# A convolution network on one core: the order of the shifted copies, and when their split is issued

## The chip, the cores and the metric

The kernel runs on one core of a Trainium2 chip. The metric is the device time of one execution in microseconds (us). Five engines matter here: TensorE (PE; its weight loads are shown as PEld), VectorE (DVE), ScalarE (ACT), GpSimd (POOL) and SyncE (SP), which issues most of the transfers. Each engine works through its own queue in order.

## The reference

Four layers, each `x = x + layer(group_norm(x))` on an image batch of 4 x 32 x 32 x 16. Layers 0, 1 and 3 are the same construction with other weights: every output position has a 3x3 convolution kernel of its own, whose result over the whole image is compared with the input and summed with weights.

```python
first = einsum('ijyx,byxc->bijc', M, inputs)
kern = transpose(G, (0, 1, 5, 4, 2, 3)).reshape(h * w * f, c, 3, 3)
shifted = conv(x_nchw, kern, 'SAME')            # 1024 positions x 16 channels, each a 32 x 32 image
diff = relu(inputs[:, None, None] - shifted)
second = einsum('ijyx,bijyxc->bijc', W, diff)
return first - second
```

Layer 2 pools intervals of the image and runs two small steps of a dynamic programme with sigmoids. It is cheap beside the others.

## The kernel before

**Phases and steps.** The batch is taken in two groups `g` of two images (`GB = 2`). The three convolution layers and two groups make six phases; layer 3 of the reference is layer index 2 of the kernel, and layer 2 of the reference is worked (`interval_layer`) inside the preparation of that one. A phase has 8 chunks of 128 output positions, and a chunk 32 steps, one for each of 16 filters and 2 images: 256 steps a phase, 1536 in all. In a step, `first_part` runs 8 matmuls into a PSUM pair (four such pairs rotate), ScalarE scales it (L614), `second_part` of the step before runs 6 more matmuls, and VectorE takes the minimum with 0, multiplies by the weights W and sums (L630).

**Precision in parts.** Weights and inputs are split into a high part and a rest, so that products keep more digits: `iy`, `iz` and `iyz` are the parts of the input for taps 0 to 7, `im9` (im in the profile) is the input for tap 8. `split` makes them: VectorE cuts the high part of both slots (`upper`, L191, upper_x in the profile), GpSimd subtracts it (L259), ScalarE scales it (L263); then `halve` (L167, ScalarE), two `difference` (L266, GpSimd) and `halve_rest` (L170, VectorE) follow.

**Weights.** `prep_parts` prepares one unit (4 filters of a chunk) in every 8 steps, spread over places 0 to 7: at place 0 the high part (VectorE L191), at 1 the ninth tap's half (ScalarE L167), at 2 L224 on ScalarE with L225 and L226 on GpSimd, at 3 L228 and L229, at 4 the next unit's subtraction (GpSimd L202), at 6 the two transfers L235, which copy the parts turned to the other half of the partitions, and the load of another unit (L107). L235 and L107 are on SyncE's queue.

**What runs behind.** The generator `behind(phase)` prepares the next phase while the current one runs: the group norm, the write of the normalised image into a padded buffer `xs` in DRAM (L346, four transfers), the shifted copies `raw` out of it (L356: 12 taps or rows, two transfers each), a wait, then the split. Slots 0 and 1 of `raw` hold taps 0 to 7, 16 partitions each for either half of the image; slot 2 holds tap 8 four times over. A positive number that the generator yields is a number of steps to wait. `IDLE` (0) waits for a step whose place in the unit allows it (0, 4, 5, 6, 7), `CALM` for place 5, 6 or 7. The order of all instructions is written out in this way; the scheduler doesn't change it. In phases 0 and 2 the split is followed by `first_terms`, 128 matmuls for the first sum of a layer (L386) and their addition. Whatever is left of `behind` at the end of a phase is issued at once.

The places where this preparation runs are reached at step 102 of phase 0 (first shifted copy), at step 38 of phases 1 and 2, and at step 210 of phases 3 and 4, where the interval layer comes first. The wait ahead of the split is 12 steps in phases 0 to 2 and 7 in phases 3 and 4.

Of the kernel before, what the change touches and what calls it, by code (L numbers as in the profile page):

```python
# [41 lines left out]
def net_kernel(ctx: ExitStack, tc: tile.TileContext, x, xq, xi, convs, iv_w, iv_b, out):  # L42
# [123 lines left out]
    def halve(dst, src, mask):  # L166
        nc.scalar.activation(dst, src, AF.Copy, scale=mask[:, 1:2])  # L167

    def halve_rest(dst, src, mask):
        nc.vector.scalar_tensor_tensor(  # L170
            dst, src, mask[:, 0:1], dst.bitcast(F32), op0=ALU.mult, op1=ALU.add
        )
# [11 lines left out]
    def image(v, x):  # L184
        return v.rearrange("... (y x) -> ... y x", x=x)[..., :H]
# [68 lines left out]
    def split(eng, g, b, name, pause=IDLE):  # L254

        high = upper(image(raw[:, :2, b], HP), 2, f"x{name}{b}")
        yield 1
        for s in range(2):
            eng.tensor_tensor(  # L259
                image(iz[g][:, s, b], H), image(raw[:, s, b], HP), image(high[:, s], H), ALU.subtract  # L260
            )
            yield pause
            nc.scalar.activation(iy[g][:, s, b], high[:, s], AF.Copy, scale=EPS)  # L263

    def difference(eng, g, b, s):
        eng.tensor_tensor(  # L266
            iyz[g][:, s, b], iy[g].bitcast(F32)[:, s, b], iz[g].bitcast(F32)[:, s, b],
            ALU.subtract,
        )
# [64 lines left out]
    def before_conv(g, layer):  # L334
        xn = work.tile([P, NT, GC], F32, tag="xn", bufs=2, name=f"xn_{g}_{layer}")
        xns[g] = xn
        yield from group_norm(g, f"c{g}{layer}", xn, 1 if layer == 2 else 4)

        nc.vector.transpose(
            xt[g][:, :, 1 : 1 + H], xn
        )
        inner = xs[g][:, HP : HP + H * HP].rearrange("p (t r n) -> p r t n", r=ROWS, n=HP)
        for r in range(ROWS):
            nc.sync.dma_start(inner[:, r], xt[g][GC * r : GC * (r + 1)])  # L346
        yield 2
        xsv = xs[g].rearrange("(b c) n -> c b n", b=GB)
        at = 0
        for slot, row, tap in [(2, row, 8) for row in range(4)] + [  # L350
            (tap // 4, tap % 4, tap) for tap in range(8)
        ]:
            for h in range(2):
                off = (HI * h + tap // 3) * HP + tap % 3
                r0 = 64 * h + C * row
                nc.sync.dma_start(  # L356
                    raw[r0 : r0 + C, slot ^ h if slot < 2 else 2, :, :RUN], xsv[:, :, off : off + RUN]
                )
            at += 1
            if at % 3 == 0:  # L360
                yield 1
        yield 7 if layer == 2 else 12
        for b in range(GB):
            yield from split(nc.gpsimd, g, b, f"{g}{layer}")
            yield IDLE
            halve(image(im9[g][:, b], H), image(raw[:, 2, b], HP), low_x)
            for s in range(2):
                difference(nc.gpsimd, g, b, s)
            yield 3
            halve_rest(image(im9[g][:, b], H), image(raw[:, 2, b], HP), low_x)  # L370
            yield 1
# [309 lines left out]
    def behind(phase):  # L681
        g, layer = phases[phase]
        if phase == 0:
            yield from rest_of_start()
            nc.scalar.dma_start(X[1], x[1])
            zeros(1)
            yield 1
            yield from constants()
        if phase + 1 < len(phases):
            g1, layer1 = phases[phase + 1]  # L690
            if layer1 == 2:
                yield from interval_layer(g1)
            terms = g1 == NG - 1 and layer1 < NL - 1
            if terms:
                mt = load_first_terms(layer1)
            yield from before_conv(g1, layer1)
            if terms:
                yield from first_terms(layer1, mt)
        if phase == len(phases) - 1:
            mt = load_first_terms(layer)  # L700
            yield 24
            yield from first_terms(layer, mt)
            yield 4
            nc.sync.dma_start(out[1 - g], X[1 - g])
# [228 lines left out]
```

## Time and profile before

| | |
|---|---|
| median of three runs | 2592.98 us (2589.51 to 2595.02) |
| the profiled execution | 2596.07 us, of it the span of the profile 2594.3 us |
| mean granted TensorE clock | 0.996 |
| matmuls of the convolutions, L584 | 394 ns each as shown, overlapping in the array |
| L630 on VectorE | 1536 x 1224 ns |
| L614 on ScalarE | 1520 x 1008 ns |
| L225, L229, L226, L202 on GpSimd, each x190 | 1293, 1302, 1292, 1051 ns |
| L259, L266 on GpSimd (split), each x20 | 1206, 1301 ns (medians) |
| L235 transfers, x380 | 384 KB, 5.0 us from issue to landing (median) |
| L356 transfers, x120 | 67.8 KB, 2.4 us from issue to landing (median) |
| first L356 of each preparation | at 187.67, 514.47, 936.55, 1654.22 and 2086.48 us |

The span is what the profiler sees, from the first instruction to the last; the execution's own time is 1.8 us longer. A busy TensorE is not TensorE at its peak, since matmuls overlap: what counts is how many of them fall into a stretch. Where the profile says that an engine waited for another, the wait stands in brackets behind the instruction, with the idle time before it. SPq is SyncE's queue issuing a transfer; the number beside it is how long the issue held the queue. The profile strips numbers from names, so raw stands for the weight loads `raw_<n>` and for the shifted copies; the line tells them apart.

### The profile page before, as it was taken

To read this page: it belongs to the slowest core of one execution; us is meant where nothing else is said; L and a number is where in the kernel's file an instruction comes from. 1 tells how busy PE (TensorE), PEld (TensorE's weight loads), DVE (VectorE), ACT (ScalarE), POOL (GpSimd) and SP (SyncE) were. 2 spreads that over 40 slices of the span, in tenths; PEclk is the share of its full clock that TensorE was granted. 3 is DMA by queue.
4 is the path that set the end of the run, shared out by engine and by line. 5 is a ranking of instruction groups with operands and counts; after the bars stand their busy time and mean duration, and the time that the engine had idled before them with its cause. 6 is when DMAs were issued, how large, how long until landed. Compare 5 with 4: busy or idle time off the path is not lost.

```text
span 2594.3 us, 56641 instructions
## 1 busy us (share of the span) xinstructions
PE 2564.1 (99%) x21906; PEld 2117.6 (82%) x21906; DVE 2080.3 (80%) x3620; ACT 1894.2 (73%) x2169; POOL 1102.6 (43%) x990
## 2 busy tenths in 40 slices
PE   8999999999999999999999999999999999999999
PEld 5997888888888887888888877798888789788887
DVE  8886777877777877777788878788888877777777
ACT  4776777777777776777777777777777777677776
POOL 3444333453333344333345554454646353333332
PEclk9999999999999999999999999999999999999999
DMA  5655444454444654444444444544444466444442
GB/s 168 185 145 143 131 131 134 121 154 130 129 137 129 195 158 111 137 129 129 131 139 131 131 124 133 151 131 124 125 132 134 127 148 195 119 139 131 131 131 52
DMA packets 81182, 353.80 MB, mean 136 GB/s; under 512 B 18448, under 2 KB 20368, under 8 KB 80144
## 3 DMA queue, kind: packets, MB, share of 16 engines
q1 hardware_dynamic: 79920, 349.57, 48.2%
q8 instruction: 172, 2.82, 0.4%
q14 instruction: 98, 0.80, 0.1%
q10 hardware_dynamic: 864, 0.58, 0.1%
q0 software_dynamic: 128, 0.02, 0.0%
HBM read 199.19 MB, written 0.98 MB: 77 GB/s over the span
## 4 chain that ended last, share of the span: by engine, by line
PE 95%; DMA 2%; issue 1%; SPq 1%; ACT 0%; POOL 0%; DVE 0%; POOLq 0%; DVEq 0%; ACTq 0%
PE pc L584 93%; DMA parts<-parts 1%; PE pf L386 1%; DMA raw<-in_g 1%; SPq L356 1%; ACT pc L614 0%; POOL parts L225 0%; POOL W L226 0%; PE ps_l L509 0%; SPq L235 0%; DVE junk L630 0%; PE ps_r L522 0%; SPq L346 0%; DMA raw<-xs 0%; POOL parts L229 0%
## 5 line engine op out<-in xcount | busy, mean ns | idle before, releaser
L630 DVE SCALAR_TENSOR_TENSOR junk<-pc,WT 128x1024 f32<-128x1024 f32 x1536 | 1879.9, 1224 | 485.0 <-PE pc L584 437.6
L614 ACT ACTIVATE pc<-pc 128x1024 f32<-128x1024 f32 x1520 | 1531.8, 1008 | 664.1 <-PE pc L584 631.0
L584 PE MATMUL pc<-iy,parts 64*128 64x512 f32 x6080 | 1063.4, 394 | 13.7 <-DMA parts<-parts 13.6
L584 PE MATMUL pc<-iyz,parts 64*128 64x512 f32 x6080 | 1059.8, 394 | 4.0 <-ACT pc L614 4.0
L584 PE MATMUL pc<-iz,parts 64*128 64x512 f32 x6080 | 1059.8, 393 | 0.0
L584 PEld LDWEIGHTS pc<-iy,parts 64*128 64x128 f32 x6080 | 664.5, 185 | 140.8 <-DMA parts<-parts 17.2
L584 PEld LDWEIGHTS pc<-iz,parts 64*128 64x128 f32 x6080 | 665.2, 185 | 121.2
L584 PEld LDWEIGHTS pc<-iyz,parts 64*128 64x128 f32 x6080 | 645.7, 185 | 111.7 <-ACT pc L614 3.7
L584 PE MATMUL pc<-im,W 64*128 64x512 f32 x3072 | 714.8, 397 | 0.0
L225 POOL TENSOR_TENSOR parts<-raw,upper_w 128x512 fp32r<-128x512 f32 x190 | 245.7, 1293 | 1091.2 <-PE pc L584 955.3
L584 PEld LDWEIGHTS pc<-im,W 64*128 64x128 f32 x3072 | 372.4, 185 | 64.0 <-issue 3.6
L229 POOL TENSOR_TENSOR parts<-parts 128x512 fp32r<-128x512 f32 x190 | 247.3, 1302 | 2.2 <-ACT parts L224 1.6
L226 POOL TENSOR_TENSOR W<-W,raw 128x512 fp32r<-128x512 f32 x190 | 245.5, 1292 | 4.6 <-ACT W L167 4.6
L202 POOL TENSOR_TENSOR raw<-raw,ident 128x512 f32<-128x512 f32 x190 | 199.6, 1051 | 60.9 <-DMA raw<-in_g 39.5
L167 ACT ACTIVATE W<-raw,low_w 128x512 fp32r<-128x512 f32 x190 | 136.1, 716 | 0.1
L630 DVE DVE_READ_ACCUMULATOR junk<-pc,WT 128x1 f32 x1536 | 127.5, 83 | 0.0
L224 ACT ACTIVATE parts<-upper_w 128x512 fp32r<-128x512 f32 x190 | 118.6, 624 | 4.2 <-DVE upper_w L191 4.2
L228 ACT CAST parts<-upper_w 128x512 fp32r<-128x512 f32 x190 | 116.7, 614 | 0.0
L191 DVE TENSOR_SCALAR upper_w<-raw 128x512 int32<-128x512 int32 x190 | 82.0, 432 | 0.0
L645 POOL TENSOR_SCALAR acc<-acc 128x32 f32<-128x32 f32 x40 | 11.5, 288 | 160.4 <-DVE junk L630 155.8
L541 POOL TENSOR_TENSOR tables<-ft_b,rt 128x1089 f32<-128x1089 f32 x16 | 37.7, 2354 | 0.4 <-DVE s_b L548 0.4
L541 POOL TENSOR_TENSOR tables<-ft_a,rt 128x1089 f32<-128x1089 f32 x16 | 37.6, 2351 | 0.0
(137 smaller groups left out, 393.0 us busy)
## 6 DMA issues: line engine op xcount, KB each, us to landing
raw<-in_g SPq DMA_DIRECT2D x190, 768.0 KB, 7.2
parts<-parts SPq DMA_DIRECT2D x380, 384.0 KB, 5.0
WT<-in_w SPq DMA_DIRECT2D x48, 512.0 KB, 4.4
MT<-in_mt SPq DMA_DIRECT2D x6, 2048.0 KB, 14.0
raw<-xs SPq DMA_DIRECT2D x120, 67.8 KB, 2.4
raw<-in_xi SPq DMA_DIRECT2D x3, 271.0 KB, 4.6
raw<-in_xi SPq DMA_DIRECT2D x1, 813.0 KB, 7.2
xs<-xt SPq DMA_DIRECT2D x20, 34.0 KB, 2.0
```

What stands on the lines that cost most here:

```text
L167: nc.scalar.activation(dst, src, AF.Copy, scale=mask[:, 1:2])
L191: nc.vector.tensor_scalar(t.bitcast(I32), src.bitcast(I32), HIGH, None, op0=ALU.bitwise_and)
L202: eng.tensor_tensor(raws[u][:, s, at:to], raws[u][:, s, at:to], pick[s][:, f0 + at : f0 + to].unsqueeze(2).to_broadcast([P, to - at, P]), ...
L224: nc.scalar.activation(WD, high, AF.Copy, scale=-EPS)
L225: nc.gpsimd.tensor_tensor(WL, w8, high, ALU.subtract)
L226: nc.gpsimd.tensor_tensor(W9, W9.bitcast(F32), src[:, 2], ALU.add)
L228: nc.scalar.copy(WU, high)
L229: nc.gpsimd.tensor_tensor(WD, WD.bitcast(F32), WL.bitcast(F32), ALU.add)
L541: nc.gpsimd.tensor_tensor(t, ft[:, i, :].unsqueeze(1).to_broadcast([P, T1, T1]), rt, ALU.add,)
L584: nc.tensor.matmul(ps[:, h, :], lhsT=w[r], rhs=v[r], start=first and k == 0, stop=k == len(pairs) - 1, skip_group_check=not first,)
L614: nc.scalar.activation(ps, ps, AF.Copy, scale=1.0 + EPS)
L630: nc.vector.scalar_tensor_tensor(junk, ps.rearrange("p h n -> p (h n)"), 0.0, chunks[n], op0=ALU.min, op1=ALU.mult, accum_out=accs[phase][ ...
```

## The change

The list of shifted copies is put in another order: taps 0 to 7 come first, and the four rows of tap 8 last. The number of transfers and the yields between them stay. The wait between the last of them and the first split becomes 12 steps instead of 7 in layer index 2, and 24 instead of 12 in the others. Nothing else is touched.

```diff
         xsv = xs[g].rearrange("(b c) n -> c b n", b=GB)
         at = 0
-        for slot, row, tap in [(2, row, 8) for row in range(4)] + [
-            (tap // 4, tap % 4, tap) for tap in range(8)
+        for slot, row, tap in [(tap // 4, tap % 4, tap) for tap in range(8)] + [
+            (2, row, 8) for row in range(4)
         ]:
             for h in range(2):
                 off = (HI * h + tap // 3) * HP + tap % 3
...
             at += 1
             if at % 3 == 0:
                 yield 1
-        yield 7 if layer == 2 else 12
+        yield 12 if layer == 2 else 24
         for b in range(GB):
             yield from split(nc.gpsimd, g, b, f"{g}{layer}")
             yield IDLE
```

## The prediction

> **What bounds the kernel now.** I read the page's busy times first, then the chain that ended last, then the busy times in 20 us windows, and then each engine's timeline around the five places where a phase's input is prepared (I call them turns: phase 1's input is prepared in phase 0, and so on up to phase 5's).
>
> From the page: TensorE is busy for all but 30 us, and the chain is its work.
>
> ```profile
> PE 2564.1 (99%) x21906; PEld 2117.6 (82%) x21906; DVE 2080.3 (80%) x3620; ACT 1894.2 (73%) x2169; POOL 1102.6 (43%) x990
> PE 95%; DMA 2%; issue 1%; SPq 1%; ACT 0%; POOL 0%; DVE 0%; POOLq 0%; DVEq 0%; ACTq 0%
> ```
>
> The windows (start:end, length, then PE busy and its matmuls, PEld, DVE, ACT, POOL, PE clock, DMA share, GB/s) show where it loses time: a full window holds 174 to 176 matmuls, the ones at the turns fewer, and the window after turn 1's stall is full.
>
> ```profile
> 180.00:200.00 20.00, 20.00 (x174) 18.38 (x172) 16.26 (x29) 15.86 (x19) 8.62 (x8) 1.00 0.45 105
> 200.00:220.00 20.00, 17.23 (x125) 13.93 (x123) 11.26 (x19) 10.37 (x12) 6.22 (x6) 0.83 0.62 167
> 220.00:240.00 20.00, 20.00 (x174) 17.51 (x172) 17.39 (x29) 17.98 (x23) 14.82 (x14) 1.00 0.55 166
> ...
> 1660.00:1680.00 20.00, 16.35 (x127) 12.58 (x125) 11.87 (x21) 11.83 (x14) 6.30 (x6) 0.93 0.74 186
> 1680.00:1700.00 20.00, 20.00 (x171) 17.93 (x171) 16.94 (x29) 16.75 (x21) 16.95 (x16) 0.99 0.50 146
> ```
>
> TensorE's timeline, from one group of products to the same of the next step, has a regular step of 1.63 us. Above it I find, in order of the turns: 5.15, 2.99 and 2.47; 3.72, 2.70 and 2.10; 4.63; 6.06 and 2.93; 6.10, 2.98 and 2.37. The excess over 1.63 is 5.7, 3.6, 3.0, 5.7 and 6.6 us: 24.6 us, nearly all that could be won outside the start and the end.
>
> What stalls it there is SyncE's queue. Its timeline in turn 1:
>
> ```profile
> 184.02 1.81 SPq L346 DMA_DIRECT2D xs<-xt  x4
> 187.67 8.23 SPq L356 DMA_DIRECT2D raw<-xs  x18
> 196.06 1.10 SPq L235 DMA_DIRECT2D parts<-parts  x2
> 197.21 1.25 SPq L107 DMA_DIRECT2D raw<-in_g  x1
> 198.51 5.33 SPq L356 DMA_DIRECT2D raw<-xs  x6
> ```
>
> The two L235 transfers turn a unit's weight parts over to the other half of the partitions. POOL had finished their source at 184.74 (L229 began at 183.44, 1.30 long), but they stand behind eighteen of the shifted copies and start at 196.06. They land at 203.51, and TensorE waits:
>
> ```profile
> 203.51 0.79 PE L584 MATMUL pc<-iy,parts 64*128 64x512 f32 x1 [2.77 <-DMA parts<-parts]
> ```
>
> In turn 4 the order is the same: all 24 copies (15.07 us of queue), then L235.
>
> **What the Trainium skill says.** "DMA: Bandwidth & Descriptors", section "Anatomy of one DMA", says that the transfer engines don't wait on semaphores: a wait is made by the issuing sequencer, before dispatch. So what stands behind a copy in SyncE's queue waits with it, as the 11.3 us of L235 here show. "TensorE: Matmul & The Clock Gate", Part 1, says that the array's clock is halved after idleness and comes back after about 3.4 us of work, in a window that runs freely. The trace agrees with the halving: steps of 2.70 to 2.99 us follow four of the stalls, and turn 3's 3.0 us stall is followed by none. "SBUF — State Buffer", "Who interferes with whom", makes VectorE and GpSimd exclude each other on a shared port; the im correction L170 (748 ns at best, 1815 ns at most) is the operation that shows it.
>
> **Part 1: the order of the taps.** Twelve taps with two transfers each are issued before and after, with a yield after every third. Each transfer writes 16 partitions (67.8 KB). Whatever its tap, a group of four goes through the rows 0, 1, 2, 3 (tap 8's four copies, taps 0 to 3, taps 4 to 7), so with tap 8 moved from first to last the sequence of partition blocks and sizes stays the same; only the slot and the source offset differ. All of them wait for the same thing (the four xs writes; 5.3 us in 3 turns). So SyncE's queue up to and with L235 is unchanged, at 0.42 us a copy plus its gap, and so are the five stalls. Cost 0. What does change is which consumer's data lands first: the split (slots 0 and 1) can start eight copies earlier, 8 x 0.466 = 3.7 us (the chain has one copy every 0.466 us), and the im copies read data that land last. In VectorE's queue the im correction now has waits of its own for tap 8, which the split's wait covered before: up to 8 semaphore instructions of about 28 ns (the median of such an instruction on L356), 0.2 us once a turn. VectorE has 1.63 - 1.31 = 0.32 us free in each step, and TensorE's four PSUM pairs let it be a step late: hidden.
>
> **Part 2: the longer wait.** I count the steps from the yields. A unit's weights take eight steps (places 0 to 7); an IDLE yield waits for places 0, 4, 5, 6 or 7. In turn 1 the first split moves from step 118 to 130 of its phase, in turns 2 and 3 from 54 to 66, in turns 4 and 5 from 221 to 226. The whole preparation ends at steps 148, 84 and 244 instead of 133, 69 and 236. All are below 256, so nothing is left over to be issued at once at the end of a phase; turns 4 and 5 keep 12 steps, 20 us, before the next phase reads their result.
>
> What the wait removes: in turns 4 and 5 the split is issued before its data are there, and VectorE, queued in order, stands still:
>
> ```profile
> 1671.39 0.69 DVE L191 TENSOR_SCALAR upper_x<-raw 128x1024 int32<-128x1024 int32 x1 [0.88 <-DMA raw<-xs]
> 2104.46 0.69 DVE L191 TENSOR_SCALAR upper_x<-raw 128x1024 int32<-128x1024 int32 x1 [2.27 <-DMA raw<-xs]
> ```
>
> Both go, 3.15 us of VectorE. But TensorE has stalled on L235 at 1672.7 and 2104.4 in any case, until 1676.82 and 2108.34, with VectorE's next products late behind it. Value 0. At most, if these holds do lengthen the last two stalls, they come down to the mean of the first three (4.1 us): 1.6 + 2.5 = 4.1 us gained. Not below that, for turns 1 to 3 have such stalls without any split near them.
>
> What it adds is another position. Before, turns 1 to 3 run a split at places 3 to 7, turns 4 and 5 at 2 to 6. After, the second image runs at 2 to 6 in all five. The first image takes its high part at place 7, its first subtraction (POOL, 1.20 us) at place 0 ahead of the next unit's L225, and then waits for place 4: iy at 4 and 5, im at 6. POOL has 4.9 us of weights and 2 x 1.2 + 2 x 1.3 = 5.0 us of split in 13.1 us, and the weights have 10 us to spare before TensorE needs them (184.74 to 200.24, less 5.0 us for the median landing): hidden. ScalarE is tighter. Its eviction (1.01 us, one each 0.92 us when back to back, with 0.62 us idle) leaves room for one 0.62 us operation per step. The weights fill places 1 to 3, the split now fills 4 to 6: six steps in a row, two of them 0.72 us. Turn 4's second image in the trace has just that pattern; the worst step of TensorE beside it is 1.71 us instead of 1.63, and turn 5's is 1.70. I take 0.07 us for each of ten images, 0.7 us, against 0.3 us of such slips now: +0.4 us.
>
> **Part 3: what follows the split.** In phases 0 and 2 the first terms (128 matmuls, 7.04 us) come 15 steps later. They are TensorE's own work in a queue with work before and behind; their weights were loaded long before. They end well ahead of the next phase's norm. Cost 0.
>
> Sum on the profiled execution: 2594.3 + 0.4 = 2594.7 us of span (2596.5 with the 1.8 us around it). The runs' median stands 3.1 us lower at 2592.98, so **2593.4 us**.
>
> **Rivals.**
> - *The holds matter* (8%): turns 4 and 5 lose their extra, 2593.0 - 4.1 = 2588.9 us. For it: they are longer stalls and hold the waits. Against it: turn 1's is as long as turn 4's, without a split near.
> - *The queue comes free* (6%): the new order lets L235 start in time, all five stalls go: 2593.0 - 24.6 = 2568.4 us. Against it: the number of copies ahead of L235 is the same.
> - *ScalarE falls behind* (12%), the slower one: six filled steps in a row leave ScalarE more than its 0.62 us late, TensorE waits for the eviction, and the clock drops for a step. One such step costs 2.99 - 1.63 = 1.36 us; with ten images 13.6 us: 2606.6 us. It decides from half a microsecond an image. For it: TensorE already waits for ScalarE six times (4.0 us). Against it: the same pattern cost 0.08 us in turn 4.
> - *Nothing that counts* (74%): 2593.4 us.
>
> **Numbers.** The before runs spread over 5.5 us, so less than about 0.2% (5.2 us) can't be told from no change. The second rival counts as faster; of the first, 3 in 100 fall beyond 0.2% and 5 within. Faster 0.09, same 0.79, slower 0.12. The range, 2588 to 2599, takes in the gain of the holds nearly whole, the run spread, and the beginning of ScalarE's case.
>
> **What would show it.** L356 is still 18 plus 6 (or 24) ahead of L235, with steps of 3.7 to 6.1 us on TensorE at the same five places; upper_x no longer waits for raw<-xs; L202 in turns 4 and 5 is no longer behind a subtraction; steps beside the splits stay below 1.75 us. I'm wrong if TensorE has new steps over 2 us some 20 us after a stall (ScalarE's or POOL's case), or if L235 starts earlier than 11 us after its source in turn 1.

## The result and the profile after

The changed kernel takes 2593.72 us (median of 12 runs, 2589.41 to 2597.91) beside 2591.49 us for the kernel before on the same chips (12 runs, 2588.86 to 2595.02). The ratio is 1.0007 with a 95% interval of 0.9998 to 1.0016: no change that can be told from none. The forecast was 2593.4 us; that it lies 0.3 us from the median is luck, since runs of one kernel lie up to 8.5 us apart.

The page and the 20 us windows of the changed kernel (start:end, length, then PE busy and its matmuls, PEld, DVE, ACT, POOL, PE clock, DMA share, GB/s):

```profile
PE 2564.2 (99%) x21906; PEld 2158.5 (83%) x21906; DVE 2084.0 (80%) x3620; ACT 1893.7 (73%) x2169; POOL 1101.9 (42%) x990
...
180.00:200.00 20.00, 20.00 (x174) 18.39 (x172) 16.29 (x28) 15.70 (x19) 8.78 (x8) 1.00 0.45 108
200.00:220.00 20.00, 17.03 (x131) 13.76 (x129) 11.56 (x21) 10.93 (x13) 5.84 (x5) 0.91 0.70 182
220.00:240.00 20.00, 20.00 (x176) 17.31 (x174) 15.98 (x27) 14.81 (x17) 6.74 (x8) 1.00 0.52 155
1660.00:1680.00 20.00, 16.83 (x129) 12.99 (x127) 11.46 (x20) 10.80 (x13) 5.31 (x5) 0.90 0.71 178
```

The hole at 200 to 220 us is there as before, 131 matmuls (125 before) where a full window has 174 to 176, and so is the one of turn 4. The window after it, 220 to 240, has lost the split: GpSimd's busy time there fell from 14.82 to 6.74 us. TensorE had no use for that. SyncE's timeline of turn 1 says why the hole stays:

```profile
184.18 1.81 SPq L346 DMA_DIRECT2D xs<-xt  x4
187.95 8.23 SPq L356 DMA_DIRECT2D raw<-xs  x18
196.34 1.11 SPq L235 DMA_DIRECT2D parts<-parts  x2
197.49 1.32 SPq L107 DMA_DIRECT2D raw<-in_g  x1
```

Eighteen copies in 8.23 us, to the hundredth what it was, then L235. Its source was finished at 184.90 (L229, 183.60 plus 1.30), so the parts start 11.4 us late, and TensorE waits:

```profile
204.00 0.49 PE L584 MATMUL pc<-iy,parts 64*128 64x512 f32 x1 [2.97 <-DMA parts<-parts]
```

In the same reading of TensorE's steps as in the prediction, the excess over 1.63 us at the five turns is 5.0, 1.5, 6.1, 6.4 and 5.7 us, 24.6 us in all before rounding. That this is the sum of before to the tenth is a coincidence: each turn's own share is another, and the sum varies by several us between executions. What did change is VectorE. The high part no longer waits; its two instructions of turns 4 and 5 stand without a bracket, behind the stall:

```profile
1685.52 0.69 DVE L191 TENSOR_SCALAR upper_x<-raw 128x1024 int32<-128x1024 int32 x1
...
2117.20 0.69 DVE L191 TENSOR_SCALAR upper_x<-raw 128x1024 int32<-128x1024 int32 x1
```

### The profile page after: what moved, and what is told of

Read it like the earlier page. It is cut to its first block, busy times and chain, and to the rows that moved or that the text cites. A ratio compares the mean times of both kernels' runs of the same rounds, so it can differ in the third digit from the quotient of the medians.

```text
span 2594.4 us, 56655 instructions
## 1 busy us (share of the span) xinstructions
PE 2564.2 (99%) x21906; PEld 2158.5 (83%) x21906; DVE 2084.0 (80%) x3620; ACT 1893.7 (73%) x2169; POOL 1101.9 (42%) x990
## 4 chain that ended last, share of the span: by engine, by line
PE 94%; DMA 2%; issue 1%; SPq 1%; DVE 0%; ACT 0%; POOL 0%; ACTq 0%; DVEq 0%; POOLq 0%
PE pc L584 93%; DMA parts<-parts 1%; PE pf L386 1%; SPq L356 1%; DMA raw<-in_g 0%; DMA raw<-in_xi 0%; ACT pc L614 0%; DVE junk L630 0%; DMA first<-in_g 0%; POOL parts L225 0%; PE ps_l L509 0%; SPq L346 0%; POOL W L226 0%; SPq L235 0%; PE ps_r L522 0%
## 5 line engine op out<-in xcount | busy, mean ns | idle before, releaser
L614 ACT ACTIVATE pc<-pc 128x1024 f32<-128x1024 f32 x1520 | 1531.8, 1008 | 665.1 <-PE pc L584 640.1
L584 PE MATMUL pc<-iy,parts 64*128 64x512 f32 x6080 | 1074.4, 394 | 13.5 <-DMA parts<-parts 13.5
L584 PE MATMUL pc<-iyz,parts 64*128 64x512 f32 x6080 | 1070.8, 394 | 4.0 <-ACT pc L614 4.0
L584 PE MATMUL pc<-iz,parts 64*128 64x512 f32 x6080 | 1070.6, 393 | 0.0
L584 PEld LDWEIGHTS pc<-iy,parts 64*128 64x128 f32 x6080 | 681.0, 185 | 129.0 <-DMA parts<-parts 17.0
L584 PEld LDWEIGHTS pc<-iz,parts 64*128 64x128 f32 x6080 | 681.5, 185 | 109.3
L584 PEld LDWEIGHTS pc<-iyz,parts 64*128 64x128 f32 x6080 | 660.3, 185 | 100.1 <-ACT pc L614 3.9
L584 PE MATMUL pc<-im,W 64*128 64x512 f32 x3072 | 725.4, 397 | 0.0
L584 PEld LDWEIGHTS pc<-im,W 64*128 64x128 f32 x3072 | 382.7, 185 | 57.9 <-issue 3.4
L229 POOL TENSOR_TENSOR parts<-parts 128x512 fp32r<-128x512 f32 x190 | 246.7, 1298 | 2.0 <-ACT parts L224 1.6
## 6 DMA issues: line engine op xcount, KB each, us to landing
MT<-in_mt SPq DMA_DIRECT2D x6, 2048.0 KB, 13.4
```

The lines of the kernel that those rows point to most:

```text
L229: nc.gpsimd.tensor_tensor(WD, WD.bitcast(F32), WL.bitcast(F32), ALU.add)
L584: nc.tensor.matmul(ps[:, h, :], lhsT=w[r], rhs=v[r], start=first and k == 0, stop=k == len(pairs) - 1, skip_group_check=not first,)
L614: nc.scalar.activation(ps, ps, AF.Copy, scale=1.0 + EPS)
```

## The experiments

The theory was that the shifted copies in SyncE's queue, ahead of the weight parts, set the stalls, and that neither the order nor the longer wait touches that queue. The rivals: two effects that cancel; VectorE's holds; the load on the transfer rings rather than the queue. The kernel before ran again beside each group of experiments: its median was 2590.38 us beside the first four (25 runs), 2590.49 us beside the lumped copies and the two short waits (9 runs), and 2591.65 us beside the last pair (23 runs). Ratios are against these.

**Each part alone.** `e1_order` is the changed list with the old waits, `e2_wait` the old list with the new waits.

```diff
# e1_order, against the changed kernel
-        yield 12 if layer == 2 else 24
+        yield 7 if layer == 2 else 12
# e2_wait, against the kernel before
-        yield 7 if layer == 2 else 12
+        yield 12 if layer == 2 else 24
```

> The new order of the taps with the waits of before (12 and 7 steps). Theory A (the issue of the copies on SyncE's queue ahead of the weight parts sets the stalls, and neither part of the change touches it): same as before, ratio 1.000 within 0.001, about 2591.5 us; five stalls at the turns of some 25 us in all; the two holds of VectorE on the high part in turns 4 and 5 (0.88 and 2.27 us before) shrink to nothing, since slots 0 and 1 land eight copies earlier. Rival B (the two parts of the change have effects of a few us that cancel): 1 to 4 us faster or slower than before, and the wait alone the other way.

> The old order of the taps with the longer waits (24 and 12 steps). Theory A: same as before, ratio 1.000 within 0.001, five stalls of some 25 us in all, no hold of VectorE on the shifted copies, TensorE's steps beside the splits at most 1.71 us. Rival B: off by 1 to 4 us, the other way than the order alone.

Measured: 2592.26 us, ratio 1.0006 (0.9997 to 1.0014), and 2593.68 us, ratio 1.0007 (0.9999 to 1.0015). Each is within what can be told from nothing, and neither goes the other way: nothing cancels. All three medians (both parts, order, wait) do lie above their own before, by 2.2, 1.9 and 3.3 us, so a cost of some 2 us isn't excluded; the three traces don't show where it would lie, for none has more stall than the profile of before. Either part alone takes away the holds on the high part in turns 4 and 5. With the order alone the instruction of turn 4 starts 16.21 us after the first copy of its turn (1652.26 to 1668.47) instead of 17.17 us (1654.22 to 1671.39): earlier by about the 0.88 us of the hold, since its eight taps are no longer the last to land. The steps beside the splits with the wait alone were 1.71 us at most, as expected. The stalls were 21.8 and 20.6 us, somewhat smaller in these two executions.

**The queue, spread.** The one edit is a yield after every tap.

```diff
             at += 1
-            if at % 3 == 0:
-                yield 1
+            yield 1
```

`e3_spread` has it on the kernel before, `e4_spread_after` on the changed one. Note what a yield does here: it sets where in SyncE's queue the copies stand between the weight transfers.

> The kernel before, with a yield after every tap instead of every third, so that two copies (0.93 us of queue) are issued in a step of 1.63 us and the weight parts find the queue nearly free. Theory A: the five stalls go, 24.6 us with the half-clock steps after them: about 2567 us, ratio 0.9905; the L235 transfers start within 3 us of their source at every turn, and TensorE has no step over 2 us at the turns. Rival C (VectorE's holds lengthen the last two stalls, the rest is transfer load): at most 4 us, 2587 us. Rival D (the transfers themselves are late because the rings are full of copies and weight loads, landing 6.9 us instead of 5.0, and the issue is not the cause): stalls shrink by half at most, about 2580 us.

> The changed kernel with the same spread, a yield after every tap. Theory A: as the spread alone, ratio 0.9905 within 0.001, since order and wait are worth nothing with or without the stalls. Rival B: differs from the spread alone by 1 to 4 us.

Measured: 2569.92 us, ratio 0.9921 (0.9906 to 0.9936), and 2570.29 us, ratio 0.9922 (0.9909 to 0.9936). TensorE has no step over 1.68 us at any turn besides the first terms themselves. The expectation was about 2567 us. The windows of the spread copies on the kernel before are full:

```profile
180.00:200.00 20.00, 20.00 (x174) 17.25 (x172) 15.88 (x28) 15.70 (x19) 8.90 (x8) 1.00 0.53 133
200.00:220.00 20.00, 20.00 (x174) 17.25 (x172) 15.86 (x27) 14.35 (x16) 6.36 (x6) 1.00 0.75 196
...
1660.00:1680.00 20.00, 20.00 (x176) 16.09 (x174) 16.23 (x29) 16.52 (x20) 12.59 (x13) 1.00 0.72 199
```

The transfers are the same and the rings are busier (0.75 of the time in 200 to 220, where the kernel before has 0.62), so full rings alone don't make the stall. They may still have a part in its size: in turn 1 of before the second weight part landed 6.9 us after its issue (196.57 to 203.46), in turn 1 of the spread both second parts took 5.0 or 5.1 us. Those 1.9 us are most of the 2.77 us for which TensorE waited there, and no run takes the two apart. SyncE's timeline of turn 1 shows two details that I had wrong:

```profile
186.85 2.63 SPq L356 DMA_DIRECT2D raw<-xs  x6
189.60 1.11 SPq L235 DMA_DIRECT2D parts<-parts  x2
190.75 1.23 SPq L107 DMA_DIRECT2D raw<-in_g  x1
192.03 11.70 SPq L356 DMA_DIRECT2D raw<-xs  x16
203.89 1.10 SPq L235 DMA_DIRECT2D parts<-parts  x2
```

First, SyncE isn't paced to two copies a step. What the yields changed is the number of copies ahead of each pair of weight parts: 6, 16 and 2 instead of 18 and 6. Second, L235 isn't within 3 us of its source: the sources end at 183.93 and 196.93, so it starts 5.7 and 7.0 us late. Both lie inside the 10 us that the weights have to spare; the 11.3 and 11.4 us of the two kernels without the spread do not. The sixteen copies take longer than sixteen times 0.46 us because one of them waits 3.2 us until the weight load L107 ahead of it has landed (SyncE's waits list it as L356 for raw<-in_g), and the first one, right behind L107, takes 1.58 us to issue; the others take 0.30 to 0.43 us, as before. The median gain, 20.5 us, is less than the 24.6 us of the profiled execution of before. The table at the end of this section suggests why: that execution was a long one, 5.7 us over the median here, and the difference between executions lies in their stalls.

**The queue, lumped.** All 24 copies in one step, the split kept at its step:

```diff
-            if at % 3 == 0:
-                yield 1
-        yield 7 if layer == 2 else 12
+        yield 11 if layer == 2 else 16
```

> The kernel before with the 24 copies issued in one step, without yields between them, and the wait made 4 steps longer, so that the split stays at its step. Theory A: in turns 1 to 3 all 24 copies stand ahead of L235 instead of 18, 6 x 0.466 = 2.8 us more of stall in each, 8.4 us in all; turns 4 and 5 have 24 ahead already and stay: about plus 8 us, ratio 1.003 (1.002 to 1.005). Rival D (load on the rings, not the queue): same transfers in the same time, no change.

Measured: 2603.90 us, ratio 1.0051 (1.0039 to 1.0064). The stalls of turns 1 to 3 are 6.7, 6.7 and 7.8 us, 21.2 us together against 12.3 us in the profile of before: plus 8.9 us, where 8.4 us were expected. Turns 4 and 5, which had all copies ahead already, have 6.1 and 5.2 us. The median is 13.4 us up rather than 8, for the same reason as above: the profile of before is one of its longer executions. TensorE waits for both L235 transfers in turn 1:

```profile
203.53 0.50 PE L582 MATMUL pc<-iy,parts 64*128 64x512 f32 x1 [3.27 <-DMA parts<-parts]
205.35 0.73 PE L582 MATMUL pc<-iy,parts 64*128 64x512 f32 x1 [1.32 <-DMA parts<-parts]
```

**What the wait and the order cover.** The wait cut to one step, with the old order (`e5_nowait`) and the new one (`e6_nowait_order`):

```diff
-        yield 7 if layer == 2 else 12
+        yield 1
```

(In `e6_nowait_order` the line replaced is the changed kernel's, with 12 and 24.)

> The kernel before with hardly any wait ahead of the split (1 step), taps in the old order. VectorE meets the first high part at step 107 in turn 1, 195 us by the trace of before, while the last copy lands near 206 us. Theory A: VectorE stands still for up to 11 us at each turn, TensorE runs out of PSUM pairs after some 3 us, and the later landing ends its stall in place of the weight parts: 3 us more in each of turns 1 to 3, some 2.6 us more in turns 4 and 5, with half-clock steps about as now: plus 10 to 20 us, ratio 1.004 to 1.008. Rival (the wait never mattered, the holds lie beside the stall whatever their length): same.

> The changed order of the taps with the same short wait (1 step). Theory A: the high part needs slots 0 and 1 alone, whose last copy is the 16th of 24, landing near 197.4 us in turn 1: VectorE is held about 2 us there, some 6 us in turns 4 and 5, less than what costs TensorE anything beside its stall: 0 to 3 us over before, ratio 1.000 to 1.001. So here the order would be worth 10 us or more, which the longer waits hide. Rival (order is worth nothing because all lands together): as the short wait with the old order.

Measured: 2634.56 us, ratio 1.0170 (1.0154 to 1.0185), and 2601.49 us, ratio 1.0041 (1.0027 to 1.0055). The direction was right and both costs were under-estimated: 44.1 us where 10 to 20 were expected, and 11.0 us where 0 to 3 were. VectorE and then TensorE in turn 1 of the short wait with the old order:

```profile
194.43 0.08 DVE L630 DVE_READ_ACCUMULATOR junk<-pc,WT 128x1 f32 x1
207.33 0.69 DVE L191 TENSOR_SCALAR upper_x<-raw 128x1024 int32<-128x1024 int32 x1 [12.81 <-DMA raw<-xs]
207.94 1.22 DVE L630 SCALAR_TENSOR_TENSOR junk<-pc,WT 128x1024 f32<-128x1024 f32 x1
```

```profile
197.68 0.41 PE L584 MATMUL pc<-im,W 64*128 64x512 f32 x2
209.22 1.22 PE L584 MATMUL pc<-iy,parts 64*128 64x512 f32 x4 [11.13 <-DVE junk L630]
```

A hold of 12.81 us reaches TensorE as 11.13 us. I had reckoned that the PSUM pairs give it two steps, 3.3 us; but after the hold VectorE must first run the high part (0.6 us until the next starts) and a product of 1.2 us before a pair is free. That 1.9 us was missing from my estimate, and the copies landed 1 us later than I had it. The traces give a rule for this kernel: in all fifteen holds of this pair and of `e8_spread_nowait` below, TensorE's wait is the hold less 1.68 us, to within 0.01 us. With the new order the hold in turn 1 is 2.37 us, and turns 1 to 3 cost what they cost before (12.4 against 12.3 us), as expected. Turns 4 and 5 have holds of 7.61 and 8.52 us instead of the 6 us expected, and stalls of 8 and 10 us.

So the order is worth 33 us if the split comes right behind the copies, and nothing that can be told behind a wait of 7 steps or more. The same pair on the spread copies, with a yield after every tap and a wait of one step:

> The spread copies with the old order of the taps and a wait of 1 step. By the spread run's trace VectorE reaches the first high part near 207.3 us in turn 1 while the last copy lands near 210.8; in turns 4 and 5 near 1660.2 and 2086.0 against 1664.3 and 2091.8. Holds of 3.5 to 5.9 us; what reaches TensorE is the hold plus 1.9 us of VectorE's own work less two steps (3.3 us), and 1.4 us of half clock after it: 3.5 to 6 us at each turn, some 15 to 20 us over the spread alone: about 2587 us, ratio 0.9985 (0.995 to 1.001). Rival (without the queue's backlog the wait is needless): 2570 us.

> The spread copies with the new order and a wait of 1 step. The last copy of slots 0 and 1 lands by 202, 1660 and 2085.5 us in turns 1, 4 and 5, ahead of the first high part: no hold, no stall: as the spread alone, 2570 us, ratio 0.992 (0.991 to 0.994). Rival (order is worth nothing): as the other one.

Measured: 2597.93 us, ratio 1.0024 (1.0017 to 1.0032), and 2573.79 us, ratio 0.9931 (0.9916 to 0.9946). The first is a miss: 28 us over the spread alone instead of 15 to 20. Its holds came out as expected, and the cost of each turn nearly so (3.7 to 6.5 us where 3.5 to 6 were expected), but five such turns are 17.5 to 30 us, and my sum was too small. The new order takes 24 us off here. With the old one the holds are 3.58 to 5.32 us; turn 1's:

```profile
213.62 0.69 DVE L191 TENSOR_SCALAR upper_x<-raw 128x1024 int32<-128x1024 int32 x1 [5.32 <-DMA raw<-xs]
...
215.51 0.73 PE L583 MATMUL pc<-iy,parts 64*128 64x512 f32 x4 [3.63 <-DVE junk L629]
```

5.32 plus 1.9 less 3.3 is 3.9, the wait is 3.63: with the term that was missing, the hold's price comes out within 0.3 us. The new order isn't quite free of holds in turns 4 and 5 (2.11 and 2.41 us, expected none), which leaves it 3.9 us behind the spread with the old wait. The spread on the kernel before, 2569.92 us, is the fastest of all; it beats both kernels.

**The account.** Subtracting the excess of TensorE's steps at the five turns from each span gives nearly one number for all eleven kernels:

| kernel | span, us | excess at the turns, us | rest, us |
|---|---|---|---|
| before | 2594.3 | 24.6 | 2569.7 |
| changed | 2594.4 | 24.6 | 2569.8 |
| order alone | 2590.5 | 21.8 | 2568.7 |
| wait alone | 2589.4 | 20.6 | 2568.8 |
| lumped | 2601.7 | 32.4 | 2569.3 |
| short wait, old order | 2632.5 | 63.8 | 2568.7 |
| short wait, new order | 2599.5 | 30.2 | 2569.3 |
| spread | 2568.1 | 0 | 2568.1 |
| spread, changed | 2568.5 | 0 | 2568.5 |
| spread, short wait, old order | 2596.8 | 27.1 | 2569.7 |
| spread, short wait, new order | 2572.5 | 2.5 | 2570.0 |

The excess is read to some 0.3 us. The rest lies within 1.9 us: all but that much of what these edits do to the time, they do at the five turns.

## Why the prediction was right, point by point

- *SyncE's queue up to L235 is unchanged by the order*: shown. 8.23 us for eighteen copies before and after, L235 11.3 and 11.4 us late, stalls at the same five places. The steps there are 3.1 to 6.3 us where 3.7 to 6.1 were forecast. That this queue is the cause is shown by the spread (stalls gone) and the lumped copies (plus 8.9 us in the three turns that got more copies ahead). One part of the reasoning put the weight wrongly: it gave the 11.3 us as an example of a wait made by the issuing engine. In the trace only 1.7 us of it is such a wait (SyncE for the xs writes); 8.23 us is the plain issue time of the copies, and most of the rest that of the xs writes.
- *The holds in turns 4 and 5 go, and are worth nothing*: shown. Either part alone removes them, and neither part alone is faster. They lay beside the stall; where a hold stands by itself, TensorE waits for its length less 1.68 us.
- *The im correction gets waits of its own*: right in kind. The source view of L170 after the change has 13 semaphore instructions in the place of 1:

```profile
L170 DVEq EVENT_SEMAPHORE  x13: 21/49/50, 19.1 to 2132.6; - x13
L170 DVE SCALAR_TENSOR_TENSOR im<-raw,low_x,im x12: 747/1650/1770, 11.0 to 2146.6; 128x512 fp32r<-128x512 f32 x12
```

  (minimum/median/maximum in ns.) That is two or three per turn, of 49 ns, where I had up to eight of 28 ns; hidden as forecast. The correction itself became slower, a median of 1650 ns instead of 1008, which the prediction hadn't said; it is hidden too. The two parts of the change do one each: the order alone has the 13 semaphore instructions and a median of 918 ns, the wait alone has one and 1642 ns. After the change all ten corrections at the turns start within 0.25 us after GpSimd has begun its L229 of 1.3 us, and take 1.63 to 1.77 us; that fits the exclusion of the two engines which the prediction named, though no run tests it.
- *Slips beside the splits, plus 0.4 us*: not refuted, and too small to be called shown. The slips are 1.70 and 1.71 us, one at each turn, five and not the ten of the forecast; the spread pair, whose runs agree better, gives 2569.92 and 2570.29 us, with ranges that overlap (2569.76 to 2571.14 and 2570.05 to 2571.89).
- *ScalarE falls behind*, the slower rival: did not happen. Six filled steps in a row cost 0.08 us, and no new step near half speed appears beside a split. The six waits for ScalarE (4.0 us) that I put in its favour are in the spread kernels as well; they have nothing to do with the split.
- *The first terms moved by 15 steps*: no cost seen. They take one step of about 9 us in every kernel.

The least sure step was the size of the stalls. I took the five stalls as fixed; in the four profiles that differ only in order and long enough wait (the first four rows of the table) their sum goes from 20.6 to 24.6 us, and the span goes with it.

## What to carry to other kernels

A wait that lies beside a longer one on another queue is worth nothing to remove: look first for what TensorE waits for last, and count what stands ahead of it in its queue. Transfers that are issued in a burst delay whatever shares their queue by their whole issue time (11.05 us for the 24 in turn 1 of the lumped copies); here a few more yields, which let the weight transfers in between them, were worth 0.8%, while their order and a longer slack behind them were worth nothing that can be told. Order and slack cover for one another. The slack is enough by itself. The new order with hardly any slack costs 11 us, and with both gone the cost is 44 us.

## What was not expected of the hardware

- Much of the scatter of the runs seems to come from the stalls. The kernel before ranges over 5.7 to 9.6 us in its groups; without the stalls four runs lie within 1.4 us (2569.76 to 2571.14). But not every stall scatters: with the short wait and the old order TensorE loses 63.8 us at the turns, and four runs lie within 1.4 us as well (2634.18 to 2635.61). What sets the difference is open.
- What follows a stall of TensorE isn't set by its length: turn 3 of before lost 3.0 us in one step and none after it, while turn 2 lost 2.1 us and then had two steps of 2.70 and 2.10 us, and turn 1 lost 3.5 us and then had two of 2.99 and 2.47 us. "TensorE: Matmul & The Clock Gate", Part 1, of the Trainium skill says that the window in which idleness is judged runs freely, so that the same kernel differs from run to run; these traces fit that, but don't show the window. The 3.4 us of work that the prediction took from there was not met: in turn 1 of before the half-speed steps last from 203.51 to about 209.5, some 6 us.
